# Order of the attention loop in a two-layer kernel: transposes between two pairs of quadrant matmuls, projections spread 4, 2, 2, 4

## The chip, the cores and the metric

The kernel runs on one core of a Trainium2 chip. A core has five engines that each take their own instructions in order: TensorE (PE, with its weight loads shown apart as PEld), VectorE (DVE), ScalarE (ACT), GpSimd (POOL) and SyncE (SP, which issues most DMAs). They wait for one another on semaphores. The metric is the device time of one execution in microseconds (us), lower is better.

## What is computed

The reference is a model of two layers on x of shape (4, 512, 128). Layer 0 normalizes x, runs a recurrent attention with a memory (16 heads of 64, segments of 64 tokens) and multiplies its output by the SiLU of a feed-forward network. Layer 1 normalizes again and does the same with another attention and a mixture of experts. The change lies in the attention of layer 0. For each batch of 4, its 8 segments follow one another:

```python
q_all = x @ Wq ; k_all = x @ Wk ; v_all = x @ Wv        # 16 heads of 64, segments of 64 tokens
def step((M, Z), (q, k, v)):
    scores = where(mask, -inf, q @ k.T * scale)
    att_dot = softmax(scores) @ v
    sq = elu(q) + 1 ; sk = elu(k) + 1
    att_mem = sq @ M / (sq @ Z.T)
    M_new, Z_new = M + sk.T @ v, Z + sk.sum(axis=-2)
    att = gate * att_mem + (1 - gate) * att_dot
    out = att @ Wo
```

## The kernel before

The program has a feed-forward stage (to about 78 us), the attention of layer 0 (`attn0`, to about 342 us, its last products inside the next stage), the experts of layer 1 and the attention of layer 1. `attn0` is one loop over n = 0 to 31: four batches of eight segments, all heads at once. The methods `mm1`, `act1`, `vec1` and `pin` (L327 to L343) keep each engine's instructions in the order in which the Python code issues them, so the order of the calls in the loop is the order of the work on PE, ACT and DVE. POOL's products and the DMAs are issued in the same loop.

A pass of the loop works on several segments at once, one ahead and one behind. Each function below is a block of work; the name in brackets is that of its PSUM tile, which is how it shows in the profile.

- `scores(n+1)` (L643, `sc`): 32 instructions on 64x64 quadrants of PE, then DVE takes the minimum with a mask into `E`. `scores_exp(n+1)` (L662) is the exponential on ACT.
- `elu_exp(n, w)` (L669): exp and relu on ACT of the projected queries (w = 0) or keys (w = 1); `elu(n, w)` (L676): DVE joins them, min(exp, 1) + relu. Both inputs are in SBUF.
- `memory(n)` (L714, `mm`): queries' elu times the memory on quadrants; DVE makes a reciprocal and a product (`rm`, `t`); POOL multiplies by the gate (L731). It needs `elu(n, 0)` and the memory that `update(n-1)` left.
- `update(n)` (L733, `mu`): transposed keys times values on quadrants; DVE adds to the memory (`mz`, L746). Left out for the last segment of a batch (n mod 8 = 7).
- `attend(n)` (L748, `dot`): exponentials times values on quadrants; DVE makes maximum, reciprocal, product and maximum of sums (`rd`, `t`, `sums`); POOL multiplies (L769) and adds (L770), which gives `att`.
- `keys(n+1)` (L692, `pk`): four 128x128 transposes of the keys' elu on PE, one copy on ACT (`sk`). Left out where n+1 is the last of a batch.
- `attended(n)` (L773, `pa`): four transposes of `att`, four copies on ACT into `attT`.
- `project(h)` (L596): twelve chunks of projections for four segments ahead: four of values (`pv`, copied to `vt` and stored to DRAM, from where `values` (L697) loads them two segments ahead), four of keys and four of queries (`pp`, copied to `pj`). Each is one PSUM bank with a copy on ACT (for the first blocks of values on DVE).
- `output(h)` (L790, `po`): 64 instructions, once in four passes (n mod 4 = 1), then DVE multiplies by the gate (`sg`) and POOL adds to x.
- `between`: pieces of the next stage that run at fixed n (norm sums at 18 and 19, scale and norm from 20 on, gate logits at 23).

Two kinds of PSUM tiles go round. `wide` (three buffers of two banks) serves sc, mm, mu, dot and po in turn, `narrow` (two buffers of one bank) serves pk, pa and all projections in turn, so a narrow block can start only when the copy of the one before last is done. The SBUF tiles of the pool have two buffers each; a third `vt` waits until the store of the first has landed.

A new set of twelve chunks begins where n mod 4 = 3 (and at n = 0). Before the change the passes n mod 4 = 3, 0, 1, 2 do 4, 4, 3 and 1 of them; the first of each pass stands between `memory` and `update`, the others at the end.

## Time and profile before

| what | value |
|---|---|
| time, median of 3 runs | 758.92 us (757.89 to 761.12) |
| profiled execution | 758.95 us, its span from first to last instruction 757.1 us |
| PE busy, whole span | 710.7 us (94%) |
| DVE, ACT, POOL busy | 507.6, 492.2, 299.5 us |
| attention loop, 92.38 to 327.50 us | 235.12 us; PE busy 214.78, ACT 166.04, DVE 150.75, POOL 130.18 |

The profile is of one execution. Lines of a timeline give the start in us from the span's beginning, the duration, engine, line of the kernel (helpers such as `mm1` have one line for all matmuls, so go by the tiles), operation, output and inputs, shapes and count; in brackets the idle time of the engine before it and what ended it. PE's blocks overlap a little, since matmuls are pipelined; distances from start to start are what adds up. A stretch's line gives its bounds and its length, then the busy time of PE, PEld, DVE, ACT and POOL with counts of instructions, the granted clock of PE, the share of the DMA engines and GB/s.

### The profile page before, as it was taken

The page shows a single profiled execution, that of the slowest core. Times are in us where ns is not written, and L with a number is a line of the kernel's source. Part 1 is how long each engine was busy: PE and PEld are TensorE (multiplying, and loading weights), DVE is VectorE, ACT ScalarE, POOL GpSimd, SP SyncE. Part 2 cuts the span into 40 slices and gives each one's busy share as a digit, 9 for nine tenths or more (in the row PEclk, how much of TensorE's full clock was granted, in tenths as well). Part 3 has the DMA queues.
Part 4 walks back from the last instruction along what each step waited for, and adds up shares of the span by engine and source line. Part 5 has one row for each costly group of instructions (what it writes and reads, how often), then busy time and mean ns, then how long its engine had stood idle before and what let it go on. Part 6 is the DMA issues. An engine that isn't in the chain of part 4 may idle for free.

```text
span 757.1 us, 23560 instructions
## 1 busy us (share of the span) xinstructions
PE 710.7 (94%) x10044; PEld 430.8 (57%) x10044; DVE 507.6 (67%) x1126; ACT 492.2 (65%) x800; POOL 299.5 (40%) x340
## 2 busy tenths in 40 slices
PE   8999799999999988899999999999999999999995
PEld 4666566877867757767576777433234433432244
DVE  7766375556567656864355643688888998777874
ACT  4433567667686775843433223998999799989850
POOL 7580045656565453773017003331251344140160
PEclk9999999999999999999999999999999999999999
DMA  7840323123132221100002550758584876759200
GB/s 180 131 121 0 109 90 101 31 87 98 32 101 58 70 73 38 40 3 1 1 1 79 185 115 1 159 185 191 129 230 139 180 164 201 192 125 216 56 16 18
DMA packets 77744, 74.71 MB, mean 99 GB/s; under 512 B 41937, under 2 KB 66801, under 8 KB 74561
## 3 DMA queue, kind: packets, MB, share of 16 engines
q1 hardware_dynamic: 75568, 71.98, 36.4%
q0 software_dynamic: 1488, 0.90, 1.0%
q8 instruction: 81, 1.33, 0.8%
q10 hardware_dynamic: 576, 0.26, 0.1%
q14 instruction: 31, 0.25, 0.1%
HBM read 50.04 MB, written 23.07 MB: 97 GB/s over the span
## 4 chain that ended last, share of the span: by engine, by line
PE 68%; ACT 15%; DVE 13%; DMA 2%; issue 2%; SPq 0%; DVEq 0%; ACTq 0%
PE eo L331 10%; PE acc L331 9%; PE pp L331 7%; ACT e L334 7%; PE ph L331 7%; PE po L331 5%; PE s L331 3%; PE b L331 3%; PE pl L331 3%; PE den L331 2%; PE pg L331 2%; PE pv L331 2%; DVE elu L679 2%; DMA vd<-vt 2%; PE pu L331 2%
## 5 line engine op out<-in xcount | busy, mean ns | idle before, releaser
L334 ACT ACTIVATE e<-s 128x1024 f32<-128x1024 f32 x126 | 124.3, 1062 | 12.7 <-PE s L331 12.1
L331 PE MATMUL acc<-e,strip 128*32 128x512 f32 x1008 | 124.5, 598 | 0.3 <-DVE e L1708 0.3
L334 ACT ACTIVATE e<-e 128x1024 f32<-128x1024 f32 x106 | 109.7, 1099 | 0.0
L334 ACT ACTIVATE h<-ph 128x1024 f32<-128x1024 f32 x32 | 32.8, 1024 | 86.4 <-PE ph L331 86.4
L731 POOL TENSOR_TENSOR t<-t,gate 128x512 f32<-128x512 f32 x32 | 49.6, 1549 | 82.8 <-DVE t L712 82.8
L331 PEld LDWEIGHTS acc<-e,strip 128*32 128x32 f32 x1008 | 28.2, 109 | 70.0 <-issue 59.5
L331 PEld LDWEIGHTS eo<-w_out,h 128*128 128x128 f32 x512 | 60.7, 192 | 12.5 <-issue 9.6
L331 PE MATMUL eo<-w_out,h 128*128 128x128 f32 x512 | 63.4, 278 | 1.6 <-DVE g L964 1.3
L331 PE MATMUL ph<-xnT,w_in 128*128 128x512 f32 x128 | 62.0, 608 | 0.0
L964 DVE SCALAR_TENSOR_TENSOR g<-eo,gw,g 128x128 f32<-128x128 f32 x112 | 31.5, 343 | 40.0 <-PE eo L331 40.0
L679 DVE SCALAR_TENSOR_TENSOR elu<-elu,up 128x512 f32<-128x512 f32 x60 | 48.3, 805 | 11.9 <-ACT up L334 11.9
L334 ACT ACTIVATE pj<-pp 128x512 f32<-128x512 f32 x64 | 38.0, 594 | 25.4 <-PE pp L331 25.4
L656 DVE TENSOR_TENSOR E<-sc,cap 128x512 f32<-128x512 f32 x32 | 22.0, 687 | 44.6 <-PE sc L331 44.6
L769 POOL TENSOR_TENSOR t<-t,gate 128x512 f32<-128x512 f32 x32 | 40.7, 1272 | 26.8 <-DVE sums L768 23.4
L331 PE MATMUL s<-q,k 64*128 64x512 bf16 x256 | 41.0, 382 | 4.5 <-ACT e L334 2.9
L770 POOL TENSOR_TENSOR t<-t,t 128x512 f32<-128x512 f32 x32 | 43.0, 1343 | 2.5
L331 PEld LDWEIGHTS <-k 64*128 64x128 bf16 x256 | 8.8, 94 | 61.1 <-issue 59.3
L1548 POOL TENSOR_TENSOR pr<-pr,pr 128x512 f32<-128x512 f32 x14 | 22.6, 1634 | 41.8 <-DVE pr L1543 41.8
L334 ACT ACTIVATE elu<-pj 128x512 f32<-128x512 f32 x60 | 37.8, 630 | 0.1
L334 ACT ACTIVATE up<-pj 128x512 f32<-128x512 f32 x60 | 37.6, 627 | 0.0
L334 ACT ACTIVATE sk<-pk 128x512 f32<-128x512 f32 x28 | 16.7, 598 | 31.6 <-PE pk L686 31.3
L331 PE MATMUL pp<-xnT,l0Wq 128*64 128x128 f32 x512 | 32.9, 277 | 2.8 <-ACT sk L334 1.7
(290 smaller groups left out, 1530.0 us busy)
## 6 DMA issues: line engine op xcount, KB each, us to landing
vd<-vt SPq DMA_DIRECT2D x32, 256.0 KB
vone<-vd SPq DMA_DIRECT2D x64, 128.0 KB
first<-qe SPq DMA_DIRECT2D x8, 1024.0 KB
second<-qf SPq DMA_DIRECT2D x16, 512.0 KB
third<-qf SPq DMA_DIRECT2D x32, 256.0 KB
qf<-qT SPq DMA_DIRECT2D x64, 64.0 KB
k<-kd SPq DMA_DIRECT2D x16, 256.0 KB
q<-qd SPq DMA_DIRECT2D x16, 256.0 KB
```

The costliest lines, as they stand in the source:

```text
L331: return self.pin(self.nc.tensor.matmul(*args, **kw))
L334: return self.pin(self.nc.scalar.activation(*args, **kw))
L656: self.vec1(nc.vector.tensor_tensor(e, ps[:, :, 0:256].rearrange("p x (hp c) -> p x hp c", hp=4), bc(bc(self.cap, 1, 4), 1, 2), ALU.min,))
L679: self.vec1(nc.vector.scalar_tensor_tensor(t, t, 1.0, up, ALU.min, ALU.add))
L731: nc.gpsimd.tensor_mul(t, t, self.gate)
L769: nc.gpsimd.tensor_mul(t, t, gate2)
L770: nc.gpsimd.tensor_add(t, t, seg[n]["t1"])
L964: self.vec1(v.scalar_tensor_tensor(acc[b][:, k, :], eo[:, k, :], w, acc[b][:, k, :], ALU.mult, ALU.add))
L1548: self.nc.gpsimd.tensor_add(self.prod1[b, m], self.prod1[b, m], t)
```

## The change

Only the body of the loop in `attn0` changes. The transposes of keys move from behind `attend` to between the pair scores, memory and the pair update, attend. The transposes of attended values go there too, ahead of the keys', and are those of two segments back instead of one; in the last pass a second call at its end catches up. The key elu on DVE comes before `scores`, the query elu after `attend`, the exponential of the scores after `update`. The chunks of a set are spread 4, 4, 2, 2 over n mod 4 = 3, 0, 1, 2, all at the end of the pass, but between the transposes and `update` where n mod 4 = 2. The output block moves from before `update` to the end of the pass.

```diff
-            each = 4 if n < 3 else (4, 3, 1, 4)[n % 4]
+            each = 4 if n < 3 else (4, 2, 2, 4)[n % 4]
             nxt = n + 1 < nseg
             more = nxt and not last(n + 1)
             if n + 2 < nseg:
                 values(n + 2)
             if nxt:
                 elu_exp(n + 1, 0)
-                scores(n + 1)
             if more:
                 elu(n + 1, 1)
+            if nxt:
+                scores(n + 1)
             memory(n)
-            for chunk in todo[:1]:
-                chunk()
+            if n > 1:
+                attended(n - 2)
+            if more:
+                keys(n + 1)
+            chunks, todo = todo[:each], todo[each:]
+            if n % 4 == 2:
+                for chunk in chunks:
+                    chunk()
+                chunks = []
+            if not last(n):
+                update(n)
             if nxt:
                 scores_exp(n + 1)
-            if n % 4 == 1 and n > 4:
-                output(n // 4 - 1)
-            if nxt:
-                elu(n + 1, 0)
-            if not last(n):
-                update(n)
             for f, *args in between.get(n - 0.5, []):
                 f(*args)
             attend(n)
-            if more:
-                keys(n + 1)
-            if n:
-                attended(n - 1)
-            for chunk in todo[1:each]:
+            if nxt:
+                elu(n + 1, 0)
+            for chunk in chunks:
                 chunk()
-            todo = todo[each:]
+            if n % 4 == 1 and n > 4:
+                output(n // 4 - 1)
             if n + 2 < nseg and not last(n + 2):
                 elu_exp(n + 2, 1)
+            if not nxt:
+                attended(n - 1)
             for f, *args in between.get(n, []):
                 f(*args)
```

## The prediction

> **What bounds the kernel now.** I read the page's engine shares first, then the busy time by stretch for one round of four passes of the attention loop (n = 8 to 11; a pass runs from one scores block to the next), then the timelines of PE, ACT, DVE and POOL there. Passes are named by n mod 4.

> Engine shares of the whole span, from the page:

> ```profile
> PE 710.7 (94%) x10044; PEld 430.8 (57%) x10044; DVE 507.6 (67%) x1126; ACT 492.2 (65%) x800; POOL 299.5 (40%) x340
> ```

> Busy time by stretch, one line for each of the passes 8 to 11: duration, then busy PE, PEld, DVE, ACT, POOL.

> ```profile
> 155.26:163.45 8.19, 7.38 (x202) 6.32 (x201) 4.45 (x10) 6.02 (x14) 3.81 (x4) 1.00 0.36 117
> 163.45:173.68 10.23, 9.98 (x251) 9.14 (x249) 4.87 (x11) 5.55 (x13) 4.98 (x5) 1.00 0.13 29
> 173.68:177.91 4.23, 4.23 (x154) 3.76 (x153) 3.04 (x6) 4.00 (x8) 2.00 (x2) 1.00 0.02 4
> 177.91:186.02 8.11, 7.69 (x145) 4.22 (x145) 6.54 (x15) 6.59 (x18) 6.72 (x5) 1.00 0.43 112
> ```

> PE carries the loop: 29.3 of 30.8 us busy in these four passes, and over the whole loop (92.38 to 327.50) 214.8 of 235.1, so about 20 us of idle PE are there to be won or added to. Where the idle time sits, in pass 8 (PE timeline):

> ```profile
> 155.26 0.69 PE L331 MATMUL sc<-pj,pj 64*64 64x64 f32 x32
> 155.78 0.65 PE L331 MATMUL mm<-mz,elu 64*64 64x65 f32 x32
> 156.36 1.09 PE L331 MATMUL pp<-xnT,l0Wk 128*64 128x128 f32 x16
> 157.38 0.70 PE L331 MATMUL mu<-vone,sk 64*64 64x65 f32 x32
> 157.90 0.65 PE L331 MATMUL dot<-vone,E 64*64 64x65 f32 x32
> 158.83 0.66 PE L686 MATMUL pk<-ident,elu 128*128 128x128 f32 x4 [0.29 <-DVE elu L679]
> 159.72 0.63 PE L780 MATMUL pa<-ident,t 128*128 128x128 f32 x4 [0.23 <-ACT pj L334]
> ```

> The transposes of keys (pk) come 3.57 us into the pass and even there wait for the key elu on DVE. What the elu waits for, in ACT's timeline (passes 8 and 9 start at 155.26 and 163.45), and below it DVE's:

> ```profile
> 156.42 0.60 ACT L334 ACTIVATE vt<-pv 128x512 f32<-128x512 f32 x1 [1.31 <-DMA vd<-vt]
> 163.57 0.60 ACT L334 ACTIVATE pj<-pp 128x512 f32<-128x512 f32 x1 [0.32 <-PE pp L331]
> 164.06 0.62 ACT L334 ACTIVATE elu<-pj 128x512 f32<-128x512 f32 x1
> 164.58 0.62 ACT L334 ACTIVATE up<-pj 128x512 f32<-128x512 f32 x1
> ```

> ```profile
> 165.23 0.69 DVE L679 SCALAR_TENSOR_TENSOR elu<-elu,up 128x512 f32<-128x512 f32 x1 [0.33 <-ACT up L334]
> ```

> In the pass after projections, ACT first copies the last projection (0.12 us into the pass), then makes exp and relu of the keys, then DVE joins them: the key elu ends at 165.92, 2.47 us into pass 9. In pass 8 the copy waits for a store (value chunk to DRAM, two vt buffers) until 156.42, and the elu ends 158.78, 3.52 us in.

> [...] The traces of all passes show program order on each engine, so a block that waits holds all behind it. [...] elu takes 0.69 us alone and 1.37 us behind a POOL product that started before it:

> ```profile
> 310.26 1.28 POOL L769 TENSOR_TENSOR t<-t,gate 128x512 f32<-128x512 f32 x1 [0.66 <-DVE sums L768]
> ```

> ```profile
> 310.73 1.37 DVE L679 SCALAR_TENSOR_TENSOR elu<-elu,up 128x512 f32<-128x512 f32 x1
> ```

> **The change, part by part.** No instruction is added or removed. Start-to-start prices of PE blocks (passes 9 and 10): sc 0.51, mm 0.58, mu 0.52, dot 0.58, pa 0.49, pk 0.55 before a quadrant block, projection chunks 1.90 for two, 2.81 for three, so 3.71 for four (another 0.90), output po 3.77; three value chunks 2.87 (122.90 to 125.77), so four 3.78. Without waits a pass is 3.23 plus its chunks. 12 chunks per round as before, so PE's own work is equal; only waits count.

> *Attended values two segments back:* POOL's add was done a pass earlier, so pa never waits. Before it waited for POOL only in the last passes (0.48 us twice, 1.28 once). Its four ACT copies end 1.48 us after pa starts (151.82 to 153.29).

> *Keys between the pairs:* pk is now due at 0.51 + 0.58 + 0.49 = 1.58 us into the pass; before, a chunk, mu and dot (2.12 us) stood ahead as cover. Behind pk on PE stand mu, dot and all chunks.
> - Pass 1: elu at 2.47, pk at 2.51, wait 0.93. Pass: 3.23 + 0.93 + 1.90 + 3.77 = 9.83; before 10.23 with three chunks. −0.40.
> - Pass 0: all four value chunks now precede it. The second starts 0.97 after the first; its copy starts 1.16 later (152.34 to 153.50), takes 0.60, and its store frees the buffer 2.32 after that (154.10 to 156.42). So the fourth copy starts 5.05 after the first chunk, 1.27 into pass 0 (before 1.16). Elu ends 3.63, pk at 3.67, wait 2.09. Pass: 3.23 + 2.09 + 3.71 = 9.03; before 8.19 in pass 8, 8.04 in pass 4.
> - Pass 2 follows the output product, which hides exp and relu: no wait for pk. But the first chunk needs pa's bank (two narrow banks in turn), free at 1.09 + 1.48 + 0.05 = 2.62 where it is due at 2.13: 0.49. Pass: 3.23 + 0.49 + 1.90 = 5.62; before 4.23. Where the next segment keeps no keys (n = 6, 14, 22) the second chunk takes that bank and nothing waits: 4.64; before 3.79.

> *Query elu after attend, and pass 2's chunks ahead of update:* in other passes the chunks after attend hide this elu. After pass 2 nothing does: mu starts 1.10 before pass 3, the memory sum can start 0.76 after (as E after sc, 155.26 to 156.02), and the five DVE operations from there to the end of sums let the next start 1.73 later (177.58 to 179.31), 0.68 for the elu: it ends 2.07 into pass 3. mm needs it, at 2.12 instead of 0.51: wait 1.61. The key elu stands behind it; sums has just released POOL's product[...] (products that overlap an elu end 1.65 to 1.73 after their start, here about 3.2), so the key elu ends 3.2 + 0.54 = 3.73 and pk waits from 3.19 to 3.77. The trace does not show this pairing: [...]if POOL's add goes ahead too 1.3 more. I take 0.58. Pass 3: 3.23 + 1.61 + 0.58 + 3.78 = 9.20; before 8.11. Without an update (n = 7, 15, 23) 8.7; before 7.43.

> *Key elu ahead of E, scores' exponential after update, output after the chunks:* E (0.69) now stands behind the key elu and ends about 4.24 in pass 0, while dot, which needs its bank, comes at 4.74: nothing, but all that E loses beyond 0.5 goes on dot. The exponential is read a pass later. The output's product on DVE (sg, 0.43) now precedes the key elu of pass 2, which ends near 1.15 and is due at 1.58: nothing. POOL's add to x is read by the next stage's norm two passes later at the earliest. Of the DMAs only the value stores move, as costed in pass 0; the value loads stay first on SP in each pass, for values stored three passes earlier.

> *Sum:* passes 4–7: 9.03 + 9.83 + 4.64 + 8.7 = 32.2 against 29.49, +2.7. 8–11: 33.7 against 30.76, +2.9. 12–15: 32.2 against 29.65, +2.6. 16–19: as 8–11, but in pass 19 eight norm operations (1.6 us, 239.51 to 241.12) stand between the two elus: 10.6; +3.7. 20–23: the norm's square root makes the key elu of pass 21 end near 5.4 (DVE went on to E only at 259.81, 4.66 in), which po no longer hides: 12.7 against 11.46; others as above: +4.4. 24–26: +1.5. 27–31, no chunks: no cover anywhere, pass 29 near 9.3 against 7.59, the rest +0.2 to +0.7 each: +2.9. 0–3: pass 3 at 9.2 against 7.45, pass 0 +1.3 for value copies on DVE, passes 1 and 2 little: +2.8. Together **+23.5 us**: span 757.1 to 780.6, and with the 1.85 around it (758.95 − 757.1) 782.4; that execution is within 0.03 of the median 758.92. Predicted 782.

> **Rivals.**
> - *Faster: the key elu is ready.* If it ended before 1.58 us of a pass and the query elu before 0.51 of pass 3, the waits of 0.93 + 2.09 + 1.61 + 0.58 vanish, a round takes 28.5 instead of 30.8, −2.3 in seven rounds: about 742. For it: half of today's 20 us idle are small waits of pk, pa and chunks on banks and the elu. Against: ACT orders exp of keys behind the last copy, with 1.75 us from there to relu's end in the trace.
> - *Less slow:* [...]no extra in the norm passes (−3), the first passes even (−2): 773; if a third of the other waits is hidden too, 768.
> - *Slower still:* waits feed on each other, POOL's add ahead of the key elu eight times (+10): 792.
> - *Nothing changes:* only if lateness on ACT and DVE just moves; ACT has slack (23 of 31 us busy), but the waits are chains, not load.

> **How the numbers follow.** 0.5% (3.8 us) is about what a measurement of this kernel can tell from no change. Forecast mechanism at 774 to 789: 0.60. Less slow, 763 to 774: 0.20. Above 789: 0.10. Within 0.5%: 0.04. Faster: 0.06. So slower 0.90. The range 768 to 790 leaves out half of the less-slow case and nearly all of the faster, same and high ones, about 0.2.

> **What would show it.** Right: pk led by "DVE elu" waits near 0.9 in pass 1 and 2 in pass 0; mm led by "DVE elu" near 1.6 in pass 3; first chunk of pass 2 waiting for attT; pa never waiting for POOL; passes near 9.0, 9.8, 5.6, 9.2. Wrong: pk without waits, or mm of pass 3 following sc at 0.51; then the time falls toward the faster rival.

## The result, and the profile after

The changed kernel takes **792.07 us** (median of 6 runs, 787.52 to 796.4) against 758.79 us (median of 6, 757.1 to 761.12): 1.044 times the time before, 95% interval 1.0398 to 1.0482. It is slower by 33 us. The forecast was slower by 23.5 us, to 782, with a range up to 790: the direction and the waits came as forecast, the size did not, and the time lies 2 us above the range. The profiled execution took 790.6 us, its span 788.8 us (before 758.95 and 757.1).

The page of the kernel after, its span, engine shares and one group of instructions (busy us, mean ns of one, then the idle time of the engine just before them and what ended it):

```profile
span 788.8 us, 23563 instructions
...
PE 718.0 (91%) x10044; PEld 440.0 (56%) x10044; DVE 508.8 (65%) x1126; ACT 495.3 (63%) x800; POOL 303.5 (38%) x340
...
L686 PE MATMUL pk<-ident,elu 128*128 128x128 f32 x112 | 19.0, 295 | 24.0 <-DVE elu L679 24.0
```

The same number of PE instructions is busy for 718.0 us instead of 710.7. And PE now stands idle for 24.0 us ahead of the keys' transposes (`pk`), waiting for the keys' elu on DVE. In the list of waits of the kernel after (us in total, times, longest), the two that the change made are

```profile
PE pk L686 <- DVE elu L679: 24.0, 23, 3.7
...
PE mm L331 <- DVE elu L679: 16.5, 10, 2.2
```

Before, `pk` waited 2.3 us for it in 6 places. What the loop costs, in the view of stretches of the kernel after (columns as before: bounds, length, busy PE, PEld, DVE, ACT, POOL, granted PE clock, DMA share, GB/s): passes 8 to 11, and then the whole loop to the start of pass 30, first of the kernel before and then of the kernel after:

```profile
161.00:171.91 10.91, 8.71 (x201) 7.81 (x200) 4.54 (x10) 6.74 (x15) 5.15 (x4) 0.84 0.28 92
171.91:181.80 9.89, 9.11 (x235) 8.27 (x233) 4.36 (x10) 7.62 (x17) 4.28 (x4) 1.00 0.13 30
181.80:187.30 5.50, 5.06 (x170) 4.58 (x172) 2.65 (x6) 2.74 (x8) 2.38 (x2) 1.00 0.01 3
187.30:196.64 9.34, 7.33 (x157) 4.23 (x149) 7.47 (x16) 5.53 (x13) 6.64 (x5) 1.00 0.36 96
```

```profile
92.42:326.77 234.35, 214.05 (x5428) 171.16 (x5428) 150.02 (x354) 165.29 (x377) 130.18 (x95) 1.00 0.25 68
...
91.83:357.87 266.04, 221.57 (x5425) 180.04 (x5425) 152.75 (x354) 169.47 (x379) 134.43 (x96) 0.95 0.21 60
```

The loop grew from 234.35 to 266.04 us, by 31.7, as much as the span (the 235.12 us given for the kernel before reach 0.7 us further). PE's idle time in it went from 234.35 − 214.05 = 20.3 to 266.04 − 221.57 = 44.5 us, by 24.2, and its busy time by 7.5 us for the same work. The ends of matmuls are modelled, so this split is rough. The granted clock of the loop fell to 0.95. So there are two effects, new waits and a slower PE.

Pass 8 beside pass 12, which has the same calls, shows both (PE timeline, after; start and duration in us, in brackets the wait):

```profile
161.00 0.69 PE L331 MATMUL sc<-pj,pj 64*64 64x64 f32 x32
161.51 0.65 PE L331 MATMUL mm<-mz,elu 64*64 64x65 f32 x32
...
164.99 0.66 PE L686 MATMUL pk<-ident,elu 128*128 128x128 f32 x4 [1.94 <-DVE elu L679]
165.58 1.15 PE L331 MATMUL mu<-vone,sk 64*64 64x65 f32 x32
166.50 1.09 PE L331 MATMUL dot<-vone,E 64*64 64x65 f32 x32
167.52 4.47 PE L331 MATMUL pp<-xnT,l0Wk 128*64 128x128 f32 x64
...
200.22 0.66 PE L686 MATMUL pk<-ident,elu 128*128 128x128 f32 x4 [1.66 <-DVE elu L679]
200.81 0.70 PE L331 MATMUL mu<-vone,sk 64*64 64x65 f32 x32
201.32 0.65 PE L331 MATMUL dot<-vone,E 64*64 64x65 f32 x32
201.90 3.76 PE L331 MATMUL pp<-xnT,l0Wk 128*64 128x128 f32 x64
```

In both the transposes wait for the key elu. In pass 8 alone what follows is slow as well: mu 1.15 instead of 0.70, dot 1.09 instead of 0.65, the four key chunks 4.47 instead of 3.76. Pass 8 took 10.92 us, pass 12 8.95 us.

```profile
128.04:131.46 3.42, 1.74 (x46) 1.27 (x40) 1.43 (x4) 3.22 (x11) 0.05 (x1) 1.00 0.42 158
131.46:134.87 3.41, 3.41 (x82) 3.29 (x76) 2.96 (x7) 1.14 (x3) 1.66 (x2) 0.50 0.21 47
162.18:165.59 3.41, 1.23 (x10) 0.85 (x11) 1.34 (x3) 3.11 (x9) 0.00 (x0) 1.00 0.40 156
165.59:169.00 3.41, 3.41 (x79) 3.29 (x80) 2.72 (x8) 1.34 (x4) 1.35 (x2) 0.50 0.16 35
196.32:199.73 3.41, 2.11 (x69) 1.44 (x68) 0.26 (x1) 2.52 (x5) 1.18 (x1) 1.00 0.52 199
199.73:203.14 3.41, 2.92 (x90) 2.69 (x92) 3.24 (x8) 2.52 (x9) 1.28 (x1) 1.00 0.13 45
230.45:233.86 3.41, 1.72 (x63) 1.31 (x65) 2.09 (x5) 3.41 (x11) 0.00 (x0) 1.00 0.41 156
233.86:237.27 3.41, 3.41 (x79) 3.26 (x72) 2.26 (x7) 1.93 (x4) 2.90 (x2) 1.00 0.37 82
```

In pass 8 the wait of 1.94 us lies whole in one window, PE is busy for 36% of it, and the next window has half the clock. In pass 12 the wait of 1.66 us is cut by the window's edge at 199.73, PE is busy for 62%, and the clock stays. In passes 4 and 16 the wait of 1.69 us lies whole in a window that is left with 51% and 50%; the first is followed by half the clock, the second not. In these four pairs the edge is near half a window.

I counted this over all fourteen profiles of this study, from 80 to 400 us of each span, on a grid of the same period laid through the clock's changes in each. Of the windows at full clock in which PE was busy for less than 48%, 31 of 32 were followed by a window at half clock; from 48 to 53%, 8 of 31; above 53%, 5 of 1179. All five hold some of the small products of the gate logits (`lp`, 8 columns wide) of pass 23; of the windows above 53% without `lp` it is none of 1142. Why these windows differ is open. The kernel before lost its clock once in the loop, the kernel after six times, in two of them for two or three windows in a row. All this is a count over these profiles, not argued from a cause. A second window at half clock can be counted too: again without the windows that hold `lp`, a half-clock window in which PE was busy for less than 80% was followed by another in 8 of 8 cases, one above 85% in 1 of 45.

### The profile page after: what moved, and what is told of

Read it like the earlier page. It is cut to its first block, busy times and chain, and to the rows that moved or that the text cites. A ratio compares the mean times of both kernels' runs of the same rounds, so it can differ in the third digit from the quotient of the medians.

```text
span 788.8 us, 23563 instructions
## 1 busy us (share of the span) xinstructions
PE 718.0 (91%) x10044; PEld 440.0 (56%) x10044; DVE 508.8 (65%) x1126; ACT 495.3 (63%) x800; POOL 303.5 (38%) x340
## 4 chain that ended last, share of the span: by engine, by line
PE 69%; DVE 14%; ACT 12%; DMA 3%; issue 1%; SPq 0%; DVEq 0%; ACTq 0%
PE eo L331 9%; PE acc L331 9%; PE pp L331 8%; ACT e L334 7%; PE ph L331 6%; PE po L331 5%; DVE elu L679 4%; PE s L331 3%; PE b L331 3%; PE pl L331 3%; PE mu L331 2%; DMA vd<-vt 2%; PE pk L686 2%; PE den L331 2%; PE dot L331 2%; PE pv L331 1%
## 5 line engine op out<-in xcount | busy, mean ns | idle before, releaser
L334 ACT ACTIVATE e<-s 128x1024 f32<-128x1024 f32 x126 | 124.4, 1062 | 12.6 <-PE s L331 12.1
L331 PE MATMUL acc<-e,strip 128*32 128x512 f32 x1008 | 124.5, 598 | 0.3 <-DVE e L1713 0.3
L334 ACT ACTIVATE e<-e 128x1024 f32<-128x1024 f32 x106 | 109.6, 1099 | 0.0
L334 ACT ACTIVATE h<-ph 128x1024 f32<-128x1024 f32 x32 | 32.8, 1025 | 84.6 <-PE ph L331 84.6
L679 DVE SCALAR_TENSOR_TENSOR elu<-elu,up 128x512 f32<-128x512 f32 x60 | 49.9, 842 | 46.2 <-ACT up L334 46.2
L731 POOL TENSOR_TENSOR t<-t,gate 128x512 f32<-128x512 f32 x32 | 40.8, 1276 | 98.7 <-DVE t L712 97.8
L769 POOL TENSOR_TENSOR t<-t,gate 128x512 f32<-128x512 f32 x32 | 53.5, 1671 | 38.1 <-DVE sums L768 35.0
L331 PEld LDWEIGHTS eo<-w_out,h 128*128 128x128 f32 x512 | 60.7, 192 | 12.5 <-issue 9.7
L331 PEld LDWEIGHTS acc<-e,strip 128*32 128x32 f32 x1008 | 28.2, 109 | 70.1 <-issue 59.5
L331 PE MATMUL eo<-w_out,h 128*128 128x128 f32 x512 | 63.4, 277 | 1.6 <-DVE g L969 1.3
L334 ACT ACTIVATE pj<-pp 128x512 f32<-128x512 f32 x64 | 38.2, 597 | 38.2 <-PE pp L331 38.0
L331 PE MATMUL ph<-xnT,w_in 128*128 128x512 f32 x128 | 61.5, 603 | 0.0
L331 PE MATMUL s<-q,k 64*128 64x512 bf16 x256 | 41.0, 382 | 4.5 <-ACT e L334 2.9
L334 ACT ACTIVATE attT<-pa 128x128 f32<-128x128 f32 x128 | 24.9, 281 | 31.9 <-PE pa L780 31.9
L770 POOL TENSOR_TENSOR t<-t,t 128x512 f32<-128x512 f32 x32 | 43.5, 1359 | 2.5
L331 PEld LDWEIGHTS <-k 64*128 64x128 bf16 x256 | 8.8, 94 | 61.2 <-issue 59.4
L686 PE MATMUL pk<-ident,elu 128*128 128x128 f32 x112 | 19.0, 295 | 24.0 <-DVE elu L679 24.0
L334 ACT ACTIVATE up<-pj 128x512 f32<-128x512 f32 x60 | 37.2, 620 | 3.9 <-DVE elu L679 3.9
L334 ACT ACTIVATE elu<-pj 128x512 f32<-128x512 f32 x60 | 37.2, 620 | 0.1
L331 PE MATMUL mm<-mz,elu 64*64 64x65 f32 x1024 | 22.0, 222 | 16.5 <-DVE elu L679 16.5
```

Source lines behind the costliest of these rows:

```text
L331: return self.pin(self.nc.tensor.matmul(*args, **kw))
L334: return self.pin(self.nc.scalar.activation(*args, **kw))
L679: self.vec1(nc.vector.scalar_tensor_tensor(t, t, 1.0, up, ALU.min, ALU.add))
L686: self.pin(nc.tensor.transpose(ps[:, hp], src[:, 2 * hp : 2 * hp + 2, :].rearrange("d a j -> d (a j)"), self.ident,))
L731: nc.gpsimd.tensor_mul(t, t, self.gate)
L769: nc.gpsimd.tensor_mul(t, t, gate2)
```

## The experiments

Each time below is a median, each ratio is to the kernel before, run on the same chip (its medians there: 757.81 to 758.44), with a 95% interval. The changed kernel was not run again beside them: differences to it are differences to its 792.07 us, and its own six runs spread over 8.9 us. Experiments with redundant work repeat products that the kernel has made, or make products that nothing reads; nothing of the computation is left out. "From the changed kernel" and "from the kernel before" say what each edit starts from.

**e1, idle time filled with repeats** (from the changed kernel). Redundant: scores run three times where n mod 4 = 3 and in the last passes, memory three to eight times in passes with a long wait.

```diff
-        def scores(n):
+        def scores(n, times=1):
...
-            for hp in range(4):
+            for hp in list(range(4)) * times:
...
-        def memory(n):
+        def memory(n, times=1):
...
-            for hp in range(4):
+            for hp in list(range(4)) * times:
...
-                scores(n + 1)
-            memory(n)
+                scores(n + 1, 3 if n > 2 and (n % 4 == 3 or n in (28, 29)) else 1)
+            memory(n, {19: 3, 21: 8}.get(n, 4 if n > 3 and n % 4 == 0 and n < 28 else 1))
```

> The changed kernel, with its scores or memory products repeated (same operands, same result, redundant work) where PE waits longest: scores 3 times in passes 3, 28 and 29, memory 4 times in passes n mod 4 = 0 from n = 4 on, 3 times in pass 19, 8 times in pass 21. The blocks that PE waits for come no sooner. Clock theory (some 10 us of the loss are PE at half clock after a long wait): pk and mm start at the same place in their passes, few half-clock stretches are left, 8 to 11 us less than the changed kernel: 781 to 784. Rival (the excess over the forecast is waiting of another kind, and the clock costs nothing): 792 as before, or more where the repeats run over the wait.

788.74 us, 1.0417 (1.0394 to 1.044); clock 0.993. The clock came back, the time hardly did: 781 to 784 was expected. Passes 4 and 8 fell from 10.38 and 10.92 to 9.56 us, pass 19 from 13.54 to 10.87. But passes 12 and 16 rose from 8.95 and 8.81 to 9.77. There the cause lies on ACT, in the changed kernel's chain ahead of the key elu: its last value copy waited longer for a store (pass 12 of this kernel begins at 195.22):

```profile
196.60 1.22 ACT L334 ACTIVATE vt<-pv 128x512 f32<-128x512 f32 x2 [2.48 <-DMA vd<-vt]
```

The first store took 3.3 us from its issue to the start of this copy, instead of 2.5. Why is open. So e1 gives back what it wins: it shows that the filled passes up to 22 do not slow down (pass 23, with its `lp` products, still did), and settles no size.

**e5, the same with other fill** (from the changed kernel). Redundant: 12 products of 128x128 behind memory in n mod 4 = 0 and at n = 19, 26 at n = 21.

```diff
-        def memory(n):
+        def memory(n, fill=0):
...
+            for _ in range(fill):
+                self.mm1(
+                    ps[:, 1, 384:512], lhsT=xnT[3][:, 0, :], rhs=self.wqkv[2][:, 0:128],
+                    start=True, stop=True,
+                )
...
-            memory(n)
+            memory(n, {19: 12, 21: 26}.get(n, 12 if n > 3 and n % 4 == 0 and n < 28 else 0))
```

> The changed kernel with PE kept busy by fewer and longer products than in the first filled run: after the memory products 12 extra 128x128 products (some 1.5 us) into unused columns of the same bank in passes n mod 4 = 0 from n = 4 on and in pass 19, 26 in pass 21; redundant work, nothing reads it. pass 3 is left alone. Clock theory: no half-clock stretch starts in passes 4, 8, 19, 21; if the value stores also land as in the changed kernel, 780 to 785. Rival (keeping PE busy buys nothing beyond what it costs): 788 to 792.

793.84 us, 1.0449 (1.0415 to 1.0482), a miss: I had taken the fill at half of what it cost. Each product became two PE instructions, and 24 of them took 2.94 us by their record, where the wait to be filled was 1.66. In pass 12 (from 199.08) `pk` then waits for nothing, but starts at 4.31 us, later than unfilled (3.58):

```profile
200.17 2.94 PE L331 MATMUL mm<-l0Wv,xnT 128*128 128x128 f32 x24
...
203.39 0.60 PE L686 MATMUL pk<-ident,elu 128*128 128x128 f32 x4
```

No pass with fill lost its clock. Passes 3 and 11, unfilled, did in this kernel (10.87 and 10.71 instead of 9.34), though they had kept it in the changed kernel: in pass 11 the wait of 1.70 us had come to lie whole in a window of the grid, in pass 3 some 1.4 us of it together with the wait of 0.3 us for `pk`.

**e6, four value buffers** (from the changed kernel).

```diff
-                t = pool.tile([P, S], F32, name=f"vt{h}_{p}_{k}", tag="vt")
+                t = pool.tile([P, S], F32, name=f"vt{h}_{p}_{k}", tag="vt", bufs=4)
```

> The changed kernel with four buffers for value chunks instead of two, so that the third and fourth copy don't wait for a store. Theory: the key elu of pass 0 ends near 2.5 us into the pass instead of 3.5, pk waits 0.8 as in pass 1 instead of 1.7 (6 to 7 passes, 6 us), and with waits under 1 us the half-clock stretches of passes 4, 8 go too (3 us): 781 to 785. Rival (the wait in pass 0 comes from elsewhere on ACT): within 2 us of the changed kernel's 792.

780.21 us, 1.0259 (1.0215 to 1.0303), 12 us less than the changed kernel. All passes n mod 4 = 0 from 4 to 20 are 7.89 us, at full clock. So the store that holds the last value copy is the cause of what pass 0's wait has beyond pass 1's, as the prediction had it. Passes 3 (10.82), 19 and 21 still slow down. In pass 19 (from 248.11), `pk` and all that follows:

```profile
253.39 1.11 PE L686 MATMUL pk<-ident,elu 128*128 128x128 f32 x4 [1.65 <-DVE elu L679]
254.43 1.15 PE L331 MATMUL mu<-vone,sk 64*64 64x65 f32 x32
...
256.37 5.21 PE L331 MATMUL pv<-l0Wv,xnT 128*128 128x512 f32 x8
```

**e12, four value buffers and a smaller fill** (from e6's kernel). Redundant: scores twice where n mod 4 = 3 (from n = 3), and, by e5's loop in `memory`, 6 products at n = 19 and 14 at n = 21.

```diff
-                scores(n + 1)
-            memory(n)
+                scores(n + 1, 2 if n > 2 and n % 4 == 3 else 1)
+            memory(n, {19: 6, 21: 14}.get(n, 0))
```

> The changed kernel with four value buffers (780.2 us measured) and PE kept busy within the longest waits that are left: scores twice in passes n mod 4 = 3, 6 extra products (1.4 us) behind memory in pass 19 and 14 in pass 21, fewer than the waits are long. Redundant work, nothing reads it. Clock theory: half-clock stretches in passes 3, 19 and 21 vanish, passes 19 near 11.5 and 21 near 13: 3 to 6 us less than with four buffers alone, 774 to 777. Rival (the first filled kernels showed no gain because the clock costs nothing): 780 or more.

775.64 us, 1.0219 (1.0191 to 1.0246): by the medians, adding PE work made the kernel 4.6 us faster than e6. The four runs of each overlap (774.6 to 777.0 here, 774.19 to 781.86 for e6), so the total alone does not settle it; the passes do. Pass 3 went from 10.82 back to 9.34, pass 19 from 13.41 to 10.69, pass 21 from 15.02 to 13.41. Blocks of pass 19 (from 244.86) in this kernel, the fill first:

```profile
248.13 1.60 PE L331 MATMUL mm<-l0Wv,xnT 128*128 128x128 f32 x12
...
250.14 0.66 PE L686 MATMUL pk<-ident,elu 128*128 128x128 f32 x4
250.72 0.70 PE L331 MATMUL mu<-vone,sk 64*64 64x65 f32 x32
```

The filled pass keeps its clock, and its 10.69 us is what the prediction's waits gave for it, 10.6. New slow windows came in unfilled passes (24 at 11.20, 28 at 6.51), so a fill that leaves some places open gives a part of its gain back.

**e2, keys' exp and relu ahead of the chunks** (from the changed kernel).

```diff
                 elu(n + 1, 0)
+            if n + 2 < nseg and not last(n + 2):
+                elu_exp(n + 2, 1)
             for chunk in chunks:
...
-            if n + 2 < nseg and not last(n + 2):
-                elu_exp(n + 2, 1)
```

> The changed kernel, with exp and relu of the keys on ACT moved ahead of the pass's last chunks (from behind them). Theory of waits: pk in passes 0 and 1 no longer waits for the key elu (0.8 and 1.7 us, 7 rounds), which takes about 18 us, and with the long waits of pass 0 most half-clock stretches go, 7 to 9 us more: 765 to 768; pass 3 still has mm waiting 1.7 us. Rival (the loss comes from the order of the PE blocks or the split of the chunks itself): no more than 5 us gained, above 786.

775.69 us, 1.0245 (1.0228 to 1.0262): −16.4 us to the changed kernel, less than expected. Passes 0 fell to 7.6 to 8.3 and passes 1 from 9.88 to 8.88, by 1.00 where the prediction's wait is 0.93; pass 3 stayed at 9.34. What did not come is in passes 19, 21, 23 and 24 (13.26, 12.37, 12.57, 11.18), beside pieces of the next stage's norm.

**e3, query elu back ahead of update** (from the changed kernel).

```diff
+            if nxt:
+                elu(n + 1, 0)
             if not last(n):
                 update(n)
...
             attend(n)
-            if nxt:
-                elu(n + 1, 0)
```

> The changed kernel, with the query elu on DVE moved back ahead of update. Theory of waits: mm of passes 3, 27 to 31 no longer waits 1.7 us for it and pk there waits 0.4 instead of 0.3: some 12 to 15 us less, 777 to 780; waits of pk in passes 0 and 1 and the half-clock stretches of pass 0 stay. Rival (mm in pass 3 then waits for the memory sum or the bank instead): at most 4 us gained, 788 or more.

780.34 us, 1.0309 (1.0277 to 1.0341), −11.7. Pass 3 fell from 9.34 to 7.66 and from 8.87 to 7.20, by the 1.7 us of its wait for the query elu. Passes 12 and 20 lost their clock here (10.68 and 10.39 instead of 8.95 and 8.78), and pass 4 kept it (8.81 instead of 10.38): the waits had moved on the grid.

**e4, both** (from the changed kernel; the two edits above).

> Both edits of the two runs before. Theory of waits: all three kinds of long waits are gone and the clock stays up; the gains add, to 745 to 755, at or below the kernel before (758.8), since the loop then has fewer waits than that. Rival: a wait on narrow banks (copies of attended values) takes their place, and it stays at 760 to 770.

764.13 us, 1.0078 (1.0048 to 1.0109), −27.9, about the sum of the two (−28.1), and short of the 745 to 755 expected. It is the rival's number, but not its cause, which was a wait on narrow banks. Pass 0 is near 7.9, 1 is 8.88, 2 is 5.50 and 3 is 7.7, passes 8 to 11 together 30.1 us where before took 30.8. The rest is pass 19 (12.84), 21 (12.37) and their neighbours: there the key elu on DVE stands behind the norm's operations, whatever ACT does. In pass 19 (from 235.43) eight of them are done at 238.63, and the elu next to them and the PE block that waits for it are

```profile
238.54 1.69 DVE L679 SCALAR_TENSOR_TENSOR elu<-elu,up 128x512 f32<-128x512 f32 x1
```

```profile
240.29 1.11 PE L686 MATMUL pk<-ident,elu 128*128 128x128 f32 x4 [3.05 <-DVE elu L679]
```

POOL's add (L770) had begun just ahead of this elu, at 238.43, and the elu took 1.69 us instead of 0.69. In pass 19 of the changed kernel the add began at 256.57 and lasted 1.26 us, and the key elu that began under it, at 256.88, took 1.50.

**e7, key elu early as well, and four value buffers** (from the changed kernel; e3's edit, e6's, and the key elu issued with its exp, so ahead of the chunks and of the pieces of the next stage).

```diff
+        elu(1, 1)
         for n in range(nseg):
...
-            if more:
-                elu(n + 1, 1)
...
             attend(n)
+            if n + 2 < nseg and not last(n + 2):
+                elu_exp(n + 2, 1)
+                elu(n + 2, 1)
             for chunk in chunks:
...
-            if n + 2 < nseg and not last(n + 2):
-                elu_exp(n + 2, 1)
```

> The changed kernel with both edits of the earlier pair (exp and relu of keys ahead of the chunks, query elu ahead of update), four value buffers, and the key elu on DVE at the end of the pass before, ahead of the pieces of the next stage. Theory: no block waits long for an elu or a store, the norm's pieces no longer stand ahead of the key elu, passes near 7.1, 8.9, 5.5, 7.2 us: 745 to 752, faster than the kernel before. Rival (copies of attended values and E behind the norm's pieces take over): 756 to 764.

749.93 us, 0.9897 (0.9878 to 0.9917): **faster than the kernel before by 1.0%**, and by 42 us than the changed one. Its loop to the start of pass 30, 7.4 us shorter than before, and, in pass 12 (from 181.57), the transposes of keys that start at 1.59 us into the pass and wait for nothing:

```profile
91.62:318.58 226.96, 208.39 (x5424) 170.97 (x5424) 149.36 (x354) 167.22 (x379) 139.42 (x95) 1.00 0.25 70
```

```profile
183.16 0.60 PE L686 MATMUL pk<-ident,elu 128*128 128x128 f32 x4
...
184.78 3.90 PE L331 MATMUL pp<-xnT,l0Wk 128*64 128x128 f32 x64
```

Pass 0 is 7.04, 1 is 8.88, 19 is 8.88; no window of the loop lost its clock. PE's places for the transposes are those of the change in full. So it was not they that cost the 33 us but the place of their producers on ACT and DVE, with the stores that hold back the last value copies. The kernel before with four value buffers was not run, so how much of the gain over it is theirs is open; its waits for the key elu, where such a gain would show first, are 2.3 us in all.

The next four each start from the kernel before and make one part of the change alone.

**e8, keys' transposes behind memory**, ahead of the first chunk.

```diff
             memory(n)
+            if more:
+                keys(n + 1)
...
             attend(n)
-            if more:
-                keys(n + 1)
```

> The kernel before with one part of the change: keys' transposes directly behind the memory products (ahead of the first chunk), all else as before. Theory: pk is due 1.1 us into a pass and waits for the key elu, which ends 2.5 (3.5 in pass 0) us in, since exp and relu stand behind the last chunk on ACT: waits of 1.4 to 2.4 us in most passes that keep keys, some 25 of them, less small waits won; with half-clock stretches 20 to 40 us slower, 780 to 798. Rival (the place of the keys alone is harmless; it is the query elu or the split that costs): under 765.

804.81 us, 1.0612 (1.0595 to 1.063): +46.6 us, more than the whole change and beyond what I expected. In the list of waits of this kernel:

```profile
PE pk L686 <- DVE elu L679: 40.6, 22, 3.2
...
PE pk L686 <- DVE rm L711: 11.2, 5, 4.9
```

Both lines are the same wait: in the five places of the second, `rm` follows the key elu on DVE, which had ended 0.15 us before `pk` began. The key elu stands later here than in the changed kernel, behind E on DVE, and `pa`, which the changed order has ahead of `pk` as a little cover, stands at the end of the pass. Eight stretches of the loop lost the clock (mean of the execution 0.975).

**e9, query elu behind attend.**

```diff
-            if nxt:
-                elu(n + 1, 0)
             if not last(n):
                 update(n)
...
             attend(n)
+            if nxt:
+                elu(n + 1, 0)
```

> The kernel before with one part of the change: the query elu on DVE behind attend. Theory: where three chunks follow attend nothing shows; where none does (passes n mod 4 = 2 and those from 27 on) memory waits some 0.5 us beyond pk and pa, which stand there in this kernel, and 1.6 where pk is left out: 4 to 10 us slower, 762 to 768. Rival (the query elu costs 1.6 us in every fourth pass wherever it is placed): 772 or more.

759.04 us, 1.0008 (0.9995 to 1.0021): no difference, a miss. Passes 7 and 11 grew by 0.74 and 0.50 us; what follows the start of pass 30 was 1.3 us shorter in the profile (429.08 instead of 430.33), where the kernel before has a window at half clock and this one has none. With `pk` and `pa` behind attend this elu has most of its cover; in the changed order it has none.

**e10, attended values two back, between memory and the first chunk.**

```diff
             memory(n)
+            if n > 1:
+                attended(n - 2)
...
-            if n:
+            if not nxt:
                 attended(n - 1)
```

> The kernel before with one part of the change: transposes of attended values two segments back, between memory and the first chunk. Theory: never late, the same work, the chunks' wait for the keys' bank may move: within 3 us, 755 to 761. Rival (copies of attended values on ACT come ahead of the others and delay them): 764 or more.

761.79 us, 1.0048 (1.0037 to 1.0059), +3.4, just beyond what I expected. Passes 3 are shorter (6.9 instead of 7.4 and 8.1), but `pk` now waits for the copies of `pa` (4.1 us for attT, in 6 places), and pass 1 is 10.86 instead of 10.22, pass 21 16.11 instead of 11.46, with a window at half clock.

**e11, the split 4, 2, 2, 4.**

```diff
-            each = 4 if n < 3 else (4, 3, 1, 4)[n % 4]
+            each = 4 if n < 3 else (4, 2, 2, 4)[n % 4]
```

> The kernel before with one part of the change: chunks split 4, 2, 2, 4 (the first still ahead of update). Theory: one chunk moves from pass 1, where it stands at the end, to pass 2; PE has the same work: within 2 us, 757 to 761. Rival (the split as such costs): 764 or more.

760.99 us, 1.0026 (1.0016 to 1.0037), +2.6 us: what pass 1 loses in work (10.22 to 9.35) pass 2 gains with a wait on top (3.80 to 5.59, 4.23 to 6.35).

The four parts alone add to 46.6 + 0.6 + 3.4 + 2.6 = 53 us, the change to 33. They do not add. The query elu costs 11.7 us only in the new order. That the key elu ahead of E, `pa` ahead of `pk` and the chunks behind take something off the keys' cost is likely, but no run has them alone.

## Why the prediction was right in its direction and short in its size

By its own steps, a pass of the kernel after at full clock against the working. The working counts from start to start; the idle time that the trace gives for the same wait is mostly 0.1 to 0.2 us shorter.

| step | predicted | measured |
|---|---|---|
| pass 1, `pk` late by; pass | 0.93; 9.83 | 0.95 (idle 0.78); 9.88 |
| pass 0, `pk` late by; pass | 2.09; 9.03 | 1.83 to 2.00 (idle 1.66 to 1.69); 8.78 to 8.95 (n = 12, 16, 20) |
| pass 2, first chunk late by; pass | 0.49; 5.62, 4.64 | 0.49 (idle 0.44); 5.50, 4.63 |
| pass 3, `mm` late by | 1.61 | 1.83 (idle 1.70) |
| pass 3, `pk` late by; pass | 0.58; 9.20, 8.7 | 0.53 (idle 0.31); 9.34, 8.87 |
| pass 19 without slow windows | 10.6 | 10.69 (e12) |
| pass 21, end of the key elu; pass without slow windows | 5.4; 12.7 | 5.35; 13.41 (e12) |

For pass 21 the sum left out the four transposes of the next stage (`lnt`) at its end, 0.6 us.

The signatures named came: `pk` led by DVE's elu, `mm` of pass 3 led by it, `pa` waiting for POOL only once, for 0.4 us (its weight load). In pass 3 (from 187.30), PE:

```profile
189.65 0.70 PE L331 MATMUL mm<-mz,elu 64*64 64x65 f32 x32 [1.70 <-DVE elu L679]
...
191.24 0.66 PE L686 MATMUL pk<-ident,elu 128*128 128x128 f32 x4 [0.31 <-DVE elu L679]
```

and DVE and POOL in the same pass:

```profile
188.82 2.36 DVE L679 SCALAR_TENSOR_TENSOR elu<-elu,up 128x512 f32<-128x512 f32 x2
```

```profile
188.96 1.67 POOL L769 TENSOR_TENSOR t<-t,gate 128x512 f32<-128x512 f32 x1 [3.16 <-DVE sums L768]
```

POOL's product overlaps the two elus, as worked out: it begins under the first, lasts 1.67 us, and the second ends 3.88 us into the pass (3.73 in the working). The two elus took 2.36 us, the first 0.68 and the second, begun under the product, 1.76 (their records overlap by 0.08). The traces of the kernels before and after hold 60 elus each. Of these 120, 27 began under a POOL operation that was running already: 25 of them ended 0.55 us after that operation's end and took up to 1.76 us, the other two, with 0.05 us of it left, took 0.68. The other 93 took 0.68 to 0.69 us.

**The step that failed** stands at the head of the working: "12 chunks per round as before, so PE's own work is equal; only waits count." PE's work was equal in instructions but not in time, since windows at half clock followed waits of half a window (in pass 8 mu took 1.15 us instead of 0.70). The prediction put this term at nothing. Its size, from passes at full and at half clock:

| pass | measured | at full clock, from | difference |
|---|---|---|---|
| 4 | 10.38 | 8.81, pass 16 | 1.57 |
| 8 | 10.92 | 9.36, pass 12 and `pk` 0.41 later | 1.56 |
| 19 | 13.54 | 10.69, e12 | 2.85 |
| 21 | 14.98 | 13.41, e12 | 1.57 |
| 23 | 12.54 | 11.86, e5 | 0.68 |
| 24 | 11.63 | 9.60, e6 | 2.03 |

(In the passes of e12, e5 and e6 `pk` starts at the same place as in the changed kernel, to 0.01 us.) Together 10.3 us. Of the loop's 31.7 us this leaves 21.4 for the waits, against 23.5 forecast, so the waits were priced well. The working's 782.4 and 10.3 make 792.7, where the profiled execution took 790.6; the other 2 us are errors of both signs, the largest in pass 22 (8.5 by the working, 7.44 measured), in the first four passes (+2.8 forecast, +2.1 measured) and in pass 21. The loss is not the same in every run: in the six runs of the changed kernel the mean granted clock goes from 0.985 to 0.968, and the run with the highest is the shortest, 787.52 us, that with the lowest the longest, 796.4. In seven passes of the profiled run (3, 4, 7, 15, 16, 20 and 28) a window was left 50 to 52% busy, on the edge, and only that of pass 4 was followed by half the clock. That the six runs differ because the grid lies elsewhere in each is my guess, not shown.

The number of the rival "slower still", 792, was met for a reason that it did not name: POOL's add ahead of the key elu, its price, cannot be in a `pk` that is 0.53 late. In this kernel the add came first only in pass 19, where the key elu behind it took 1.50 us. "Less slow", whose 773 is 782 less 4 for passes 3 without the wait of `pk`, 3 for the norm's passes and 2 for the first ones, fell with the 0.53 of `pk` and the mm wait of 1.70. "Faster" fell too, yet e7 shows that its condition was the right one: with both elus ready in time passes 8 to 11 take 29.1 us, not far from the 28.5 that it worked out, and the kernel 749.93 against its 742.

## What to carry to other kernels

Price a new wait on PE twice: its length, and, where it can leave PE busy for less than about half of a 3.413 us window, as here, some 1.6 us more for what then runs at half clock (1.57 and 1.56 us for one window, in passes 4 and 8). Before a consumer is moved forward on its engine, move its producers on the other engines by as much; the same order of transposes on PE cost 33 us with late elus and won 8 with early ones and two more value buffers. Parts of such a reordering do not add up, so test them in the order they will have, not only alone.

## What was not expected of the hardware

- In the fourteen profiles the granted clock of PE was 0.50 after most 3.413 us windows of a grid in which PE was busy for less than about half (31 of 32 below 48%, 8 of 31 from 48 to 53%, 5 of 1179 above). In the changed kernel an idle time of 0.78 us in pass 1 was never followed by it; a single one of 1.7 us was only where it lay whole in a window, and two such in pass 19 were though the grid cut both.
- Redundant PE work made passes faster: pass 19 took 10.69 us with it (e12) and 13.41 without (e6).
- The extra 128x128 float32 products cost twice what I assumed: each became two instructions, and 24 of these took 2.94 us, about 0.12 us each.
- The copy that waits for a value store started 2.1 to 2.7 us after the store's issue in the changed kernel and 2.2 to 3.3 us after it in e1, with the same stores. The cause is open.
